# Two attention layers on one core: the third product of a split step in the second layer is issued one step later

## The chip, the cores and the metric

The kernel runs on one core of a Trainium2 chip. The metric is the device time of one execution in microseconds, the median of the runs shown.

## The reference, cut to what matters

Two self-attention layers run one after the other over x of shape (4, 64, 64, 256): 4 images of 4096 tokens with 256 channels. All is fp32, and each layer attends over all 4096 tokens of its image.

```python
# layer 0
q, k, v = x @ Wq + bq, x @ Wk + bk, x @ Wv + bv        # 32, 32 and 256 columns
x = gamma * (softmax(q @ k.T) @ v) + x
# layer 1
f, g, v = x @ Wf + bf, x @ Wg + bg, x @ Wh + bh        # 32, 32 and 128 columns
x = x + (softmax(g @ f.T) @ v) @ Wo + bo
```

## The kernel before, in words

`fast_path` (L239) does all the work; `general_path` (L76) is a fallback that these inputs don't take.

**Steps.** The attention is cut into steps `Step(b, l, j, i)` (L513): image, layer, query block, group of keys. In the second layer (l = 1) a query block has 512 queries, there are 8 such blocks an image (32 in all), and each has 16 steps of two key tiles of 128. A step has these parts:

- `scores` (L522): two TensorE matmuls (L529) write a 128 x 1024 tile `st` in PSUM, keys on the partitions. The pool `ps_st` (L261) has one buffer, so the next scores wait until ScalarE has read these. ScalarE then makes `p` = exp(st) (L541), and in a split step `high` = exp(st - a little), rounded to fp32r, ahead of it (L539).
- `cut_low` (L549): in a split step VectorE makes `low` = p - high (L552).
- `cut_both` (L554): in a split step VectorE makes `d` = high - 4096 low (L557). In the second layer `low` and `d` take turns in the same two buffers (tag "l"; L267, L551, L556).
- `add_up` (L561): VectorE adds p to the running sum for the softmax, except in steps 0, 3, 7, 10 and 13, for which POOL issues an adding DMA (L547).
- `products_second` (L585): the products of the exponentials with v, at L595. A step that isn't split has one product, "whole": two fp32 matmuls of p, into the accumulator `acc[1]`. A split step has three products of two fp32r matmuls each: "h" (high) and "l" (low), both into `acc[0]`, and "d" into `acc[1]`. At the end of the block the two accumulators are joined (`end_second`, L641), multiplied by Wo and divided by the sums.

In the second layer, steps 1, 4, 6, 9, 11 and 14 are split (`SPLIT1`, L68), the ten others are not. No two split steps are neighbours. In the first layer every step is split, with its own products at L577; it isn't touched.

**Order.** The main loop (L726 on) writes the steps out by hand, two ahead: at step n VectorE gets d(n), low(n+1) and the sum of n; then the scores of n+2, side work that `plan` (L693) puts at this step, and the products of n. The side work is the end of the block before (matmuls L658 and L659, in steps 1 to 4) and, in images 0 to 2, the projections of the next image (matmuls L421 and L463). `acc` is a fresh pair of PSUM banks for every block. The source gives the rank of the work; the framework sets each engine's order when the kernel is built, and the trace shows scores in the middle of the products of another step.

Of the kernel before, what the change touches and what calls it, by code (L numbers as in the profile page):

```python
# [238 lines left out]
def fast_path(ctx: ExitStack, tc: tile.TileContext, x, w0, w1, wo, bo, gamma, out, off):  # L239
# [26 lines left out]
    def wide(tag, name, dtype=F32):  # L266
        return work.tile([P, 2 * QB], dtype, tag=tag, bufs={"d": 1, "e": 1, "p": 3}.get(tag, 2), name=name)  # L267
# [226 lines left out]
    def load_q(b, l, j, cols=slice(0, QB), parts=None):  # L494
        if (b, l, j) not in q_t:
            q_t[b, l, j] = data.tile([P, QB], F32R, tag="q", bufs=2, name=f"q_{b}_{l}_{j}")
        parts = qk_dram[b, l, j].bitcast(F32R) if parts is None else parts
        load_rows(q_t[b, l, j][:, cols], parts, 0, (0, 0, 1, 1))

    def load_k(b, l, j, cols=slice(0, QB), parts=None):  # L500
        if (b, l, j) not in k_t:
            k_t[b, l, j] = data.tile([P, QB], F32R, tag="k", bufs=NB, name=f"k_{b}_{l}_{j}")
        parts = qk_dram[b, l, j].bitcast(F32R) if parts is None else parts
        load_rows(k_t[b, l, j][:, cols], parts, 1, (0, 1, 0, 1))
# [4 lines left out]
    def small(name):  # L509
        return work.tile([P, C], F32, tag="small", bufs=4, name=name)  # L510


    class Step:  # L513
# [71 lines left out]
        def products_second(self, acc, parts):  # L585
            v = v_t[self.b, self.i]
            for part in parts:
                p, v_part, which, first, last = {
                    "h": lambda: (self.high, v["h"], 0, self.i == SPLIT1[0], False),
                    "l": lambda: (self.low, v["l"], 0, False, self.i == SPLIT1[-1]),  # L590
                    "d": lambda: (self.d, v["d"], 1, self.first, self.last),
                    "whole": lambda: (self.p, v, 1, self.first, self.last),
                }[part]()
                for g in range(G[1]):
                    nc.tensor.matmul(  # L595
                        acc[which],
                        v_part[:, g, :],
                        p[:, g * QB : (g + 1) * QB],
                        start=first and g == 0,
                        stop=last and g == G[1] - 1,  # L600
                    )
# [39 lines left out]
    def end_second(b, j, acc, p_sum):  # L641
        key = f"{b}_{j}"
        o = []
        for h in range(QB // QB0):
            part = slice(h * QB0, (h + 1) * QB0)
            o.append(work.tile([P, W], F32, tag="o", name=f"o_{key}_{h}"))
            nc.scalar.activation(o[h][:, :QB0], acc[0][:, part], AF.Copy, scale=1.0 + EPS)
            nc.vector.tensor_add(o[h][:, :QB0], o[h][:, :QB0], acc[1][:, part])
        sums = work.tile([P, QB], F32, tag="sums", bufs=1, name=f"sums_{key}")
        nc.vector.tensor_add(p_sum, p_sum, moved_sums[b, j])  # L650
        nc.vector.tensor_add(sums, p_sum[:, :QB], p_sum[:, QB:])

        def output(t):
            def issue():
                tok = slice(t * P, (t + 1) * P)
                ps = side_psum(f"pso_{key}_{t}")
                part = o[t // NS][:, t % NS * P : (t % NS + 1) * P]
                nc.tensor.matmul(ps[:, :C], part, wo_sb, start=True, stop=True)  # L658
                nc.tensor.matmul(ps[:, C : C + 1], sums[:, tok], ones[:, :1], start=True, stop=True)  # L659
                n = (b * N + j * QB) // P + t  # L660
                nc.vector.reciprocal(inverse[:, 1, n : n + 1], ps[:, C : C + 1])

                y = small(f"y_{key}_{t}")
                nc.scalar.activation(y, ps[:, :C], AF.Copy, scale=inverse[:, 1, n : n + 1])  # L664
                row = j * QB + t * P
                nc.gpsimd.dma_start(out[b, row : row + P, :], y, accum_op=ALU.add)  # L666

            return issue

        return [output(t) for t in range(NT)]  # L670

    def run(units):
        for u in units:
            u()
# [9 lines left out]
    steps = [Step(b, l, j, i) for b in range(B) for l in range(2) for j in range(NQ[l]) for i in range(NI[l])]  # L684
# [6 lines left out]
    acc, p_sum, units = None, None, {}  # L691

    def plan(b, l, j, ends):  # L693

        units = {}

        def put(i, *some):
            units.setdefault(i, []).extend(some)

        if l == 0:  # L700

            if j >= 2:
                t, qk, v = project_units(b, 1, j - 2)
                put(0, t), put(4, qk), put(5, v)
            for n, u in enumerate(ends):
                put(1 + n, u)
            return units
        if j == 0:
            for n, u in enumerate(ends):
                put(1 + n, u)  # L710
            for n, h in enumerate((NH - 2, NH - 1)):
                t, qk, v = project_units(b, 1, h)
                put(6 * n, t), put(6 * n + 2, qk), put(6 * n + 3, v)
        else:
            for n, u in enumerate(ends):
                put(1 + n, u)
        if b + 1 < B:
            for h in range(NH):
                i = 12 + 7 * h - j * NI[1]
                for n, u in zip((0, 2, 3), project_units(b + 1, 0, h)):  # L720
                    if 0 <= i + n < NI[1]:
                        put(i + n, u)
        return units

    ends = bias_units()
    for n, s in enumerate(steps):  # L726
        b, l, j = s.b, s.l, s.j
        if s.first:
            units = plan(b, l, j, ends)
            acc = [  # L730
                ps_acc.tile([P, QB], F32, tag="acc", name=f"acc_{b}_{l}_{j}_{a}") for a in range(2 * NS if l == 0 else 2)
            ]
            if l == 1:
                p_sum = wide("d", f"p_sum_{b}_{j}")
        if l == 0 and s.last:
            x_res[b, j] = []
            for t in range(NS):
                x_res[b, j].append(small(f"x_res_{b}_{j}_{t}"))
                row = (j * NS + t) * P
                nc.sync.dma_start(x_res[b, j][t], x[b, row : row + P, :])  # L740
                nc.gpsimd.tensor_add(x_res[b, j][t], x_res[b, j][t], bv)  # L741

        ahead = steps[n + 3] if n + 3 < len(steps) else None
        if ahead is not None and ahead.first:
            k = (ahead.b, ahead.l, ahead.j * (QB0, QB)[ahead.l] // QB)
            if k not in q_t:
                load_q(*k)
        if b == l == j == 0 and s.i == 5:
            load_q(0, 0, 0, slice(QB0, QB), qk_dram[0, 0, 0].bitcast(F32R)[:, :, :, QB0:])
        after, later = (steps[n + k] if n + k < len(steps) else beyond for k in (1, 2))  # L750

        early = []
        if b == l == j == 0 and s.i + AHEAD < NB:
            early = [project_units(0, 0, 2 * (s.i + AHEAD) + k) for k in range(2)]
            run([u[0] for u in early])

        s.cut_both()
        after.cut_low()
        s.add_up(p_sum)
        todo = units.get(s.i, [])  # L760

        if l == 1:
            later.scores()
            run(todo)
            s.products_second(acc, ("h", "l", "d") if s.split else ("whole",))
        else:
            for half, what in ((0, "h"), (0, "l"), (1, "h")) if s.last else ((0, "h"), (1, "h")):
                s.products_first(acc, half, what)
            for half in () if s.last else (0, 1):
                s.products_first(acc, half, "l")  # L770
            if early:
                run(early[0][1:] + early[1][1:])
            later.scores()
            run(todo)
            for half, what in ((0, "d"), (1, "l"), (1, "d")) if s.last else ((0, "d"), (1, "d")):
                s.products_first(acc, half, what)

        over = (min(s.i + 2, NI[l] - 1) + 1) * G[l] // NT if j == NQ[l] - 1 else 0
        while keys and halves.get(keys[0]) == 2 and (keys[0][:2] == (b, l) or keys[0][2] < over):
            load_k(*keys.pop(0))  # L780
        if s.last:
            ends = end_first(b, j, acc) if l == 0 else end_second(b, j, acc, p_sum)
# [70 lines left out]
```

## Time and profile before

| what | value |
|---|---|
| median of 3 runs | 3232.82 us (3232.46 to 3236.61) |
| the profiled execution, its own time | 3232.26 us |
| its span in the trace | 3230.1 us, 2.2 us less |
| granted TensorE clock | 0.997 |
| busy: TensorE, VectorE, ScalarE, POOL | 98%, 83%, 66%, 28% |
| second layer: first whole product, image 0 and last d product, image 3 | 521.2 us and 3207.9 us after the start |
| one query block of the second layer, image 3 (3093.42 to 3132.65) | 39.2 us |

Times in the profile are microseconds from the start of the span unless marked ns. PE is the TensorE matmul, PEld its weight load, DVE VectorE, ACT ScalarE, SP the engine whose queue issues DMAs. A group's line gives the source line, engine, operation, output and inputs, shape and count, then busy time, mean ns of one, and the idle time of the engine just before, with what ended it. A matmul's record is longer than the distance to the next one, since matmuls are pipelined; a weight load carries the wait for its matmul's data, and the idle time before it is shown in brackets. Below, d(6) stands for the d product of step 6, whole(7) for the whole product of step 7, and so on; score 0 and score 1 at a block's end belong to the next block.

### The profile page before, as it was taken

The numbers are of one execution on the slowest core, as the hardware profiler recorded it, in microseconds if no ns is written. First come the engines' busy times: TensorE is split into PE (matmuls) and PEld (weight loads), VectorE is DVE, ScalarE is ACT, GpSimd is POOL, SyncE is SP. The second block draws the span as 40 slices with busy tenths as digits, with TensorE's granted clock in tenths as the row PEclk, the third lists the DMA queues.
The fourth block names the chain that finished last, engine by engine and source line by source line (L and its number), as shares of the span: only waits on it lengthen the run. The fifth ranks groups of instructions, "written<-read, shape, count | busy, mean of one in ns | idle before, by whom it ended". The sixth has DMA issues, their size and how long they took to land.

```text
span 3230.1 us, 54167 instructions
## 1 busy us (share of the span) xinstructions
PE 3159.7 (98%) x19908; PEld 2653.3 (82%) x19908; DVE 2679.5 (83%) x3237; ACT 2146.8 (66%) x2835; POOL 898.9 (28%) x1108
## 2 busy tenths in 40 slices
PE   8999999999999999999999999999999999999997
PEld 7999997666799999666689999966668999995554
DVE  7888888888788888888878888888888888887775
ACT  7666666767666666677766666667776666666664
POOL 5222223222422223322232222422233222232221
PEclk9999999999999999999999999999999999999999
DMA  4111214555421122555531111345562121134443
GB/s 120 45 45 48 52 46 105 105 102 105 93 50 46 46 52 54 107 107 103 110 76 47 45 47 47 73 101 108 103 117 61 42 52 48 45 87 89 85 87 66
DMA packets 391391, 239.49 MB, mean 74 GB/s; under 512 B 266672, under 2 KB 355248, under 8 KB 391120
## 3 DMA queue, kind: packets, MB, share of 16 engines
q0 software_dynamic: 68160, 134.86, 21.4%
q1 hardware_dynamic: 322048, 100.76, 13.0%
q8 instruction: 161, 2.64, 0.3%
q14 instruction: 110, 0.90, 0.1%
q10 hardware_dynamic: 912, 0.33, 0.0%
HBM read 82.58 MB, written 67.11 MB: 46 GB/s over the span
## 4 chain that ended last, share of the span: by engine, by line
PE 83%; DVE 6%; issue 4%; ACT 4%; DMA 2%; SPq 1%; POOL 0%; DVEq 0%; ACTq 0%; POOLq 0%
PE acc L577 44%; PE acc L595 18%; PE st L529 13%; PE psv L463 4%; DVE d L557 2%; DVE low L552 2%; ACT p L541 2%; PE psqk L421 2%; PE pso L658 1%; ACT high L539 1%; DMA squares<-x_dram 1%; SPq L279 1%; DMA squares<-in_x 1%; PE pso L659 0%; DMA p_sum_moved<-p 0%
## 5 line engine op out<-in xcount | busy, mean ns | idle before, releaser
L539 ACT ACTIVATE high<-st,down 128x1024 fp32r<-128x1024 f32 x704 | 786.2, 1117 | 734.5 <-PE st L529 532.8
L541 ACT ACTIVATE p<-st 128x1024 f32<-128x1024 f32 x1024 | 1045.8, 1021 | 230.8 <-PE st L529 225.3
L552 DVE TENSOR_TENSOR low<-p,high 128x1024 fp32r<-128x1024 f32 x704 | 937.5, 1332 | 192.4 <-ACT p L541 191.7
L557 DVE SCALAR_TENSOR_TENSOR d<-low,high 128x1024 fp32r<-128x1024 f32 x704 | 865.6, 1230 | 235.2 <-PE acc L577 232.3
L529 PE MATMUL st<-q,k 128*128 128x256 f32 (+1 forms) x3072 | 742.9, 349 | 10.0 <-ACT p L541 6.6
L595 PE MATMUL acc<-p,v 128*128 128x512 f32 x1280 | 614.7, 594 | 0.0
L529 PEld LDWEIGHTS st<-q,k 128*128 128x128 f32 x3072 | 454.4, 189 | 187.8 <-ACT p L541 122.7
L577 PE MATMUL acc<-v0d,d 128*128 128x258 f32 x4096 | 593.6, 284 | 3.1 <-DVE d L557 2.8
L577 PE MATMUL acc<-v0h,high 128*128 128x258 f32 x4096 | 590.8, 284 | 1.2 <-ACT high L539 1.2
L577 PE MATMUL acc<-v0l,low 128*128 128x258 f32 x4096 | 589.0, 283 | 0.1
L577 PEld LDWEIGHTS acc<-v0h,high 128*128 128x128 f32 x4096 | 535.3, 190 | 3.1 <-issue 1.4
L577 PEld LDWEIGHTS acc<-v0d,d 128*128 128x128 f32 x4096 | 530.4, 189 | 6.1 <-DVE d L557 5.3
L577 PEld LDWEIGHTS acc<-v0l,low 128*128 128x128 f32 x4096 | 532.9, 190 | 0.6 <-DVE low L552 0.3
L634 POOL TENSOR_TENSOR x_res<-x,bo 128x256 f32<-128x256 f32 x128 | 198.7, 1552 | 877.8 <-DVE x L623 877.7
L595 PEld LDWEIGHTS acc<-p,v 128*128 128x128 f32 x1280 | 236.3, 189 | 148.8 <-issue 123.2
L570 DVE TENSOR_TENSOR p_sum<-p_sum,p 128x1024 f32<-128x1024 f32 x288 | 350.3, 1216 | 8.2 <-ACT p L541 5.8
L547 POOL DMA_DIRECT2D p_sum_moved<-p x128 | 113.1, 884 | 527.0 <-ACT p L541 425.5
L492 POOL DMA_DIRECT2D q<-qk_dram x256 | 127.9, 510 | 323.7 <-PE st L529 318.5
L463 PE MATMUL psv<-wv,xT 128*128 128x128 f32 (+1 forms) x1024 | 202.2, 330 | 1.8 <-DVE v0d L481 1.4
L741 POOL TENSOR_TENSOR x_res<-x_res,bv 128x256 f32<-128x256 f32 x128 | 181.5, 1419 | 66.6 <-DMA x_res<-in_x 66.0
L463 PEld LDWEIGHTS psv<-wv,xT 128*128 128x128 f32 x1024 | 158.4, 191 | 32.6 <-issue 14.6
L666 POOL DMA_DIRECT2D out<-y x128 | 116.7, 930 | 243.0 <-ACT y L664 220.1
(100 smaller groups left out, 2411.7 us busy)
## 6 DMA issues: line engine op xcount, KB each, us to landing
p_sum_moved<-p POOLq DMA_DIRECT2D x160, 512.0 KB, 4.6
x_res<-in_x SPq DMA_DIRECT2D x128, 128.0 KB, 2.1
qk_dram<-qk_parts SPq DMA_DIRECT2D x128, 128.0 KB, 1.9
x_dram<-x SPq DMA_DIRECT2D x128, 128.0 KB, 1.7
out<-x_res SPq DMA_DIRECT2D x128, 128.0 KB, 1.7
squares<-x_dram SPq DMA_DIRECT2D x512, 32.0 KB, 1.9
out<-y POOLq DMA_DIRECT2D x128, 128.0 KB, 3.4
q<-qk_dram POOLq DMA_DIRECT2D x252, 64.0 KB, 2.3
```

What stands on the lines that cost most here:

```text
L463: nc.tensor.matmul(ps[:, t, :], xT[key][:, c, t * P : (t + 1) * P], wv[l][:, c, :], start=(c == 0), stop=(c == NCC - 1),)
L492: nc.gpsimd.dma_start(dst[n * D : (n + 1) * D, :], parts[h, which])
L529: nc.tensor.matmul(st[:, g, :], k_t[b, l, kt // NT][:, kt % NT * P : (kt % NT + 1) * P], q_t[b, l, j * n // QB][:, q0 : q0 + n], start=Tru ...
L539: nc.scalar.activation(self.high, s_flat, AF.Exp, bias=down)
L541: nc.scalar.activation(self.p, s_flat, AF.Exp)
L552: nc.vector.tensor_sub(self.low, self.p, self.high.bitcast(F32))
L557: nc.vector.scalar_tensor_tensor(self.d, self.low.bitcast(F32), -UP, self.high.bitcast(F32), ALU.mult, ALU.add)
L570: nc.vector.tensor_add(p_sum, p_sum, self.p)
L577: nc.tensor.matmul(acc[2 * s + which][:, :W], p[:, g * QB0 + s * P : g * QB0 + (s + 1) * P], v0[self.i][v][:, g, :], start=self.first and ...
L595: nc.tensor.matmul(acc[which], v_part[:, g, :], p[:, g * QB : (g + 1) * QB], start=first and g == 0, stop=last and g == G[1] - 1,)
L634: nc.gpsimd.tensor_add(x_old[s], x_new[s], bo_sb)
L741: nc.gpsimd.tensor_add(x_res[b, j][t], x_res[b, j][t], bv)
```

## The change

In a split step of the second layer, "d" is taken out of the call that issues the products. It is issued in the next step instead, which is never split: behind that step's whole product, or ahead of it where that step is the last of the block (step 15, for the d of step 14). The whole product of step 0 still opens acc[1] and that of step 15 still closes it; the flags of d, which depended on being the first or last step, become constants.

```diff
-                    "d": lambda: (self.d, v["d"], 1, self.first, self.last),
+                    "d": lambda: (self.d, v["d"], 1, False, False),
...
         if l == 1:
             later.scores()
             run(todo)
-            s.products_second(acc, ("h", "l", "d") if s.split else ("whole",))
+
+            behind = steps[n - 1] if not s.first and steps[n - 1].split else None
+            if s.last and behind:
+                behind.products_second(acc, ("d",))
+            s.products_second(acc, ("h", "l") if s.split else ("whole",))
+            if not s.last and behind:
+                behind.products_second(acc, ("d",))
```

## The prediction

> **What bounds the kernel now.** I read the page first (busy shares, then the chain that ended last), then the groups by form, then who waited for whom on TensorE, then one stretch of the second layer in order of time.
>
> ```profile
> PE 3159.7 (98%) x19908; PEld 2653.3 (82%) x19908; DVE 2679.5 (83%) x3237; ACT 2146.8 (66%) x2835; POOL 898.9 (28%) x1108
> PE 83%; DVE 6%; issue 4%; ACT 4%; DMA 2%; SPq 1%; POOL 0%; DVEq 0%; ACTq 0%; POOLq 0%
> ```
>
> TensorE is busy nearly all the time and is 83% of the chain, so only its idle time can be won. The next lines are three groups of second-layer products (columns: count, then busy us and mean ns of one, then idle time before), and one line of the waits on TensorE.
>
> ```profile
> L595 PE MATMUL acc<-p,v 128*128 128x512 f32 x1280 | 614.7, 594 | 0.0
> L595 PE MATMUL acc<-high,v 128*128 128x512 f32 x384 | 146.3, 461 | 2.0 <-ACT high L539 2.0
> L595 PE MATMUL acc<-d,v 128*128 128x512 f32 x384 | 130.3, 420 | 25.7 <-DVE d L557 23.6
> ...
> PE acc L595 <- DVE d L557: 23.6, 40, 1.5
> ```
>
> The moved product is the only one on L595 with a wait worth naming. Its 23.6 us is too low, because matmul records overlap. In the trace the end of one 512-column fp32r matmul follows the end of the one before by 0.231 us, and each of the four passes that a whole fp32 product (two matmuls) leaves by 0.428 us. What the ends lie further apart is idle. Summed by that rule over the trace, counting gaps over 40 ns, TensorE idles ahead of the d products by split step (32 query blocks): step 1 2.8 us, 4 none, 6 7.9, 9 7.2, 11 10.2, 14 15.4. The first five make 28.1 us: 15.7 in images 0 to 2 together, 12.4 in image 3, which has no projection work for a next image beside it.
>
> One block of image 3 in order of time (start, duration, what; idle before):
>
> ```profile
> 3115.17 1.22 DVE L557 SCALAR_TENSOR_TENSOR d<-low,high 128x1024 fp32r<-128x1024 f32 x1
> 3115.45 0.63 PE L595 MATMUL acc<-low,v 128*128 128x512 f32 x2
> ...
> 3116.44 0.30 PEld L595 LDWEIGHTS acc<-d,v 128*128 128x128 f32 x2 [0.80 <-DVE d L557]
> 3116.44 0.73 PE L595 MATMUL acc<-d,v 128*128 128x512 f32 x2 [0.36 <-DVE d L557]
> 3116.71 1.02 ACT L541 ACTIVATE p<-st 128x1024 f32<-128x1024 f32 x1
> ...
> 3117.01 1.88 PE L595 MATMUL acc<-p,v 128*128 128x512 f32 x4
> ...
> 3118.33 1.03 PE L529 MATMUL st<-q,k 128*128 128x512 f32 x2
> ...
> 3120.47 0.30 PEld L529 LDWEIGHTS st<-q,k 128*128 128x128 f32 x2 [0.63 <-ACT p L541]
> 3121.24 1.03 ACT L541 ACTIVATE p<-st 128x1024 f32<-128x1024 f32 x1 [0.82 <-PE st L529]
> 3121.31 0.30 PEld L595 LDWEIGHTS acc<-d,v 128*128 128x128 f32 x2 [0.54 <-DVE d L557]
> ```
>
> See that d(9) is made by VectorE from 3115.17 on, that TensorE has done low(9) and stands, and that the whole product of step 10, whose p has been ready for some time, follows only after it. See also the second limit: a score waits for ScalarE's p, because st has one buffer (L261, L526), so scores and exponentials alternate. In this block (3093.42 to 3132.65, 39.2 us) seven of the 16 scores start 0.16 us after the p before them ended; there ScalarE, not TensorE, sets the pace.
>
> **What the Trainium skill says.** "TensorE: Matmul & The Clock Gate", Architectural detail: TensorE pulls weight loads ahead of matmuls, but matmuls stay in order, and VectorE and ScalarE are strict FIFO. The trace agrees: at 3116.44 the load for d waits, and the ready whole product behind does not pass it. So only the order of the instructions can fill that hole. "Perfetto Trace Analysis", Tensor Engine Instruction: the end of a matmul record is estimated, which is why I use spacing; the trace agrees, records of 395 ns (median for low) lie 231 ns apart. "PSUM — Partial Sum Buffer", The four PSUM rules: the first matmul of a group clears, the others add. Step 0 opens and step 15 closes acc[1], both whole products and neither split, so the changed flags on d do nothing.
>
> **The change part by part.**
>
> Work removed or added: none. 384 d matmuls stay, 6 x 32 pairs at 0.462 us. No DMA is issued by the moved call, so the POOL and SP queues keep their order; POOL's copies of p (L547) hang on ScalarE. On TensorE it is moved past the scores and side units of step n+1 and its whole product.
>
> Steps 1, 4, 6, 9, 11: d(n) goes behind the whole product of n+1. What stood behind the wait was the scores of n+3 and that whole product, 1.71 us. That is longer than the longest wait seen (1.2 us in these steps), so where p is ready the hole is filled. What is late next is the score. I walk the block above with the durations of the trace: p's end to score 0.155, score's end to ScalarE 0.22, VectorE's end to d 0.16.
> - Step 6: low(6) stops at 3109.17 and d(6) waits 0.39. But score 9 can't start before 3110.11, since p(8) ends at 3109.95. Half of whole(7), 0.857, fits in between. Score 9 gains nothing; score 10 gains 0.13, its slack (start 3113.15, p(9) ended 3112.86).
> - Step 9: scores and low(9) are 0.13 earlier, low(9) ends 3115.78. Whole(10) runs to 3117.50. p(11), also 0.13 earlier, ends 3117.60, so score 12 starts 3117.75 instead of 3118.72: 0.97 gained. d(9) follows it.
> - Step 11: score 13 hangs on p(12), so 3119.60 instead of 3120.57. Whole(12) goes before d(11) and ends 3121.78; score 14 starts then instead of 3122.73: 0.95 kept, nothing more.
> - Step 14: d(14) stays ahead of whole(15) and only changes places with the score and side units of step 15. Its 15.4 us hangs on VectorE's low(14), sum, d(14), which start when p(14) ends. I count zero of it, with bounds 0 and 15.4.
> So the block gains 0.96 of the 1.40 us that its d products idle in the five steps: 69%. Step 4 has no wait; step 1 has 0.9 us or less an image.
>
> Image 3: 8 blocks x 0.96 = 7.7 us. Images 0 to 2: the idle times sit in fewer blocks beside projection matmuls; 0.69 x 15.7 = 10.8. Sum 18.5 us.
>
> Buffers: d and low share tag "l" with two buffers (L267), so d(6) is written where d(4) was, and d(11) where d(9) was. In the block d(4)'s product ended at 3105.56 and VectorE began d(6) at 3108.19, 2.6 us later. With whole(5) in between (1.71), and the 0.46 of d(4) itself behind it, it ends about 3107.8 plus 0.16: margin 0.2. Where side units stand in step 5 or 10 (a query/key projection, 0.47 us by four matmuls 0.117 apart, or a value projection, 8 x 0.215 = 1.72 us), VectorE waits, and low(n) and the sums queue behind that. By plan (L717 to L722) such units fall there in four of the eight blocks of images 0 to 2, 12 cases. Nothing in before shows this wait. From below 0; a gain is excluded, since a later release helps nobody. From above about 1.7 us each, 20 us. Much of it is cover, since d itself now has 1.71 us more time. I take 2 us.
>
> Order: the engines don't run in source order. Scores stand in the middle of whole products in the trace, so the build ranks what is ready and the source gives only the rank. In none of the 192 split steps does a whole product pass an earlier d, so d blocks whole as read above, and after the change d(n) stays behind whole(n+1). Where exactly the scores fall is unknown; I price it at zero, 0.2 us a block either way (6 us).
>
> Sum: 3232.26 (profiled execution: span 3230.1 and 2.2 around it) - 18.5 + 2.0 = 3215.8; the median shown is 0.56 above that execution: 3216.3.
>
> **The rivals.**
> 1. Part of the wait is won (above): 3216. For: the filler is ready and long enough. Chance 0.44.
> 2. All of it: the chain from the scores has more slack in the blocks with projections than in the one I walked. 3232.8 - 28.1 = 3204.7. Against: the scores that start right behind p. Chance 0.11.
> 3. The wait moves: at each d the score waits for ScalarE instead, as in step 6, or the build leaves d where it was because it counts it as ready. Then 3232, within 0.2%. For: ScalarE is the releaser of seven scores of 16. Chance 0.19.
> 4. Slower: VectorE's d(6) and d(11) wait for the released buffer of d(4) and d(9), and low(9), low(14) and the sums queue behind. There are 64 such pairs; from 18.5 / 64 = 0.29 us on average they eat the gain. At 0.4 us, 25.6 - 18.5 = 7 us slower: 3240. For: margin 2.6 to 0.2 us, VectorE busy 83%. Against: in the block VectorE stands idle 8.4 us for ScalarE. Chance 0.26.
>
> **Numbers.** Faster 0.55 (1 and 2), same 0.19, slower 0.26; the bound of 0.2% (6.5 us) is about what a measurement of this kernel can tell from no change. The range reaches from most of case 2 (3206) to case 4 at its price (3240); some 0.05 lies below, 0.13 above. The likeliest case alone has 3209 to 3223, by the 6 us of order and the buffer wait.
>
> **What would show it.** Right: idle time ahead of d in steps 1, 6, 9 and 11 falls below 5 us in sum, the image-3 block shrinks from 39.2 to about 38.3 us, score 12 starts within 0.3 us of the end of p(11), and step 14 keeps its wait. Wrong: the wait of scores for p (6.6 us in the view of who waited for whom) grows by as much as d's falls (case 3), or d L557 shows a wait for acc L595, which it never does now (case 4).

## The result, and the profile after

| | before | after |
|---|---|---|
| median of 8 runs each | 3232.64 us (3230.55 to 3236.61) | 3225.61 us (3222.68 to 3227.84) |
| ratio after / before | | 0.9976, 95% interval 0.9965 to 0.9986 |
| the profiled execution, its own time | 3232.26 us | 3224.69 us |
| its span, granted TensorE clock | 3230.1 us, 0.997 | 3222.8 us, 0.997 |
| second layer, first whole(0) to last whole(15), images 0, 1, 2, 3 | 337.4, 337.0, 337.7, 317.4 us | 336.1, 336.5, 337.7, 313.9 us |
| one query block of image 3, whole(0) to the next whole(0) | 39.2 us | 38.54 us |

The change wins 7.0 us, 0.2%; 16.5 us had been forecast. The second layer gives 5.3 us in the profiled executions, 1.8 us in images 0 to 2 and 3.5 us in image 3. The four stretches ahead of the images' second layers, start and first layer, were 1.1, 1.3 and 0.4 us shorter and 0.9 us longer; the change does not touch them.

First the same lines of the page of after (busy shares, then the chain):

```profile
PE 3162.2 (98%) x19908; PEld 2651.3 (82%) x19908; DVE 2675.7 (83%) x3237; ACT 2147.8 (67%) x2835; POOL 897.1 (28%) x1108
PE 91%; DVE 3%; ACT 2%; issue 2%; DMA 1%; POOL 0%; SPq 0%; ACTq 0%; DVEq 0%; POOLq 0%
```

The number of TensorE instructions is unchanged. VectorE's share of the chain fell from 6% to 3%, TensorE's rose from 83% to 91%. Next the second-layer products of after by form (count, busy us and mean ns, idle before):

```profile
L595 PE MATMUL acc<-p,v 128*128 128x512 f32 x1280 | 623.1, 597 | 0.0
...
L595 PE MATMUL acc<-d,v 128*128 128x512 f32 x384 | 168.7, 511 | 4.4 <-DVE d L557 4.4
L595 PE MATMUL acc<-high,v 128*128 128x512 f32 x384 | 138.3, 436 | 0.4 <-ACT high L539 0.4
```

The idle time of the d group fell from 25.7 to 4.4 us. Its busy time rose from 130.3 to 168.7 us for the same 384 matmuls: a d now starts right behind a fp32 pass and its record overlaps that one. By the spacing rule of the prediction (gaps over 40 ns), the idle time ahead of d fell from 43.5 to 5.5 us, all of it in step 14; in steps 1, 4, 6, 9 and 11 no such gap is left. So the change does what it says. What it does not do is turn 38 us of filled holes into 38 us. The view of who waited for whom tells why. These are the weight loads of before (us, times, longest):

```profile
PEld st L529 <- ACT p L541: 122.7, 345, 1.6
PEld acc L595 <- DVE d L557: 52.5, 70, 2.0
```

and these the weight loads of after:

```profile
PEld st L529 <- ACT p L541: 162.8, 385, 1.5
PEld acc L595 <- DVE d L557: 7.1, 8, 2.0
```

The wait for d lost 45.4 us and the wait of the scores for p gained 40.1 us. On the matmuls themselves d went from 23.6 to 4.4 us and the score from 6.6 to 13.4 us. By the spacing rule TensorE's idle time ahead of the second layer's scores grew from about 35 to about 60 us.

Where the change works as it was walked can be seen in one block of image 3, steps 9 to 12 of after (start, duration, what):

```profile
3070.02 1.22 DVE L557 SCALAR_TENSOR_TENSOR d<-low,high 128x1024 fp32r<-128x1024 f32 x1
3070.18 0.63 PE L595 MATMUL acc<-low,v 128*128 128x512 f32 x2
...
3070.64 1.88 PE L595 MATMUL acc<-p,v 128*128 128x512 f32 x4
...
3071.44 1.02 ACT L541 ACTIVATE p<-st 128x1024 f32<-128x1024 f32 x1
...
3071.96 0.79 PE L595 MATMUL acc<-d,v 128*128 128x512 f32 x1
...
3072.59 0.42 PE L529 MATMUL st<-q,k 128*128 128x512 f32 x1
```

VectorE makes d(9) from 3070.02 on, and TensorE goes from low(9) straight into whole(10), then d(9). p(11) ends at 3072.46 and score 12 starts 0.13 us behind it.

### The profile page after: what moved, and what is told of

The parts are those of the page before. It is cut to its first block, busy times and chain, and to the rows that moved or that the text cites. A ratio compares the mean times of both kernels' runs of the same rounds, so it can differ in the third digit from the quotient of the medians.

```text
span 3222.8 us, 54179 instructions
## 1 busy us (share of the span) xinstructions
PE 3162.2 (98%) x19908; PEld 2651.3 (82%) x19908; DVE 2675.7 (83%) x3237; ACT 2147.8 (67%) x2835; POOL 897.1 (28%) x1108
## 3 DMA queue, kind: packets, MB, share of 16 engines
q1 hardware_dynamic: 322048, 100.76, 13.1%
## 4 chain that ended last, share of the span: by engine, by line
PE 91%; DVE 3%; ACT 2%; issue 2%; DMA 1%; POOL 0%; SPq 0%; ACTq 0%; DVEq 0%; POOLq 0%
PE acc L577 45%; PE acc L595 23%; PE st L529 15%; PE psv L463 4%; PE pso L658 2%; PE psqk L421 2%; ACT p L541 1%; DVE low L552 1%; DVE d L557 1%; ACT high L539 1%; PE pso L659 0%; DMA squares<-x_dram 0%; DMA k<-qk_parts 0%; DMA gamma<-in_L_conv_gamma 0%; POOL k L492 0%
## 5 line engine op out<-in xcount | busy, mean ns | idle before, releaser
L557 DVE SCALAR_TENSOR_TENSOR d<-low,high 128x1024 fp32r<-128x1024 f32 x704 | 865.4, 1229 | 235.5 <-PE acc L577 231.8
L529 PE MATMUL st<-q,k 128*128 128x256 f32 (+1 forms) x3072 | 737.1, 348 | 17.4 <-ACT p L541 13.4
L595 PE MATMUL acc<-p,v 128*128 128x512 f32 x1280 | 623.1, 597 | 0.0
```

Of the source, the lines that this page charges most:

```text
L529: nc.tensor.matmul(st[:, g, :], k_t[b, l, kt // NT][:, kt % NT * P : (kt % NT + 1) * P], q_t[b, l, j * n // QB][:, q0 : q0 + n], start=Tru ...
L557: nc.vector.scalar_tensor_tensor(self.d, self.low.bitcast(F32), -UP, self.high.bitcast(F32), ALU.mult, ALU.add)
L595: nc.tensor.matmul(acc[which], v_part[:, g, :], p[:, g * QB : (g + 1) * QB], start=first and g == 0, stop=last and g == G[1] - 1,)
```

## The experiments

**How the blocks were read.** A block's time is the distance from its first whole(0) to the next block's. All `st` tiles share one buffer, so the block can be written as 16 round trips, from the start of a score over its exponentials to the end of its p, plus 0.155 us, plus what the next score starts later than that. A score that waits gets its record early, so its start is taken as the end of its first matmul less 0.395 us, the length of a record that didn't wait. A round trip is 1.84 us in a plain step and 2.90 in a split one; ten and six of them make 35.8 us, and no block of image 3 came under that. What is above it is mostly **lateness** of scores; the rest is round trips that take longer. For the block of before (39.23 us), by score: 4: 0.22, 6: 0.99, 7: 0.39, 10: 0.14, 12: 0.84, 14: 0.30, 15: 0.14, 1: 0.17, 2: 0.14, in all 3.3 us.

**The theories.** A, with which the first group went in: idle time ahead of d is what a move wins, and what is missing of it is lost at the block's end, where the build now puts score 1 ahead of d(14). The rival, which became theory C: filled holes count only where they make a score less late, and the build's new order makes other scores late, so each block should come out as its round trips and its lateness. Images are timed in one profiled execution of each kernel. Images 0 to 2 of the two kernels at the end of group 3, where nothing in them differs from before, came out 0.6 us shorter and 1.2 us longer than before in sum, so differences near 1 us say little there. Line numbers in some of these kernels are one higher than in before, for an added line.

### Group 1: one step at a time, and the block's end

`e1_only14` moves d(14) alone, `e3_only9` d(9) alone:

```diff
+MOVED_D = (14,)        # e3_only9: (9,)
-            behind = steps[n - 1] if not s.first and steps[n - 1].split else None
+            behind = steps[n - 1] if not s.first and steps[n - 1].split and steps[n - 1].i in MOVED_D else None
...
-            s.products_second(acc, ("h", "l") if s.split else ("whole",))
+            s.products_second(acc, (("h", "l") if s.i in MOVED_D else ("h", "l", "d")) if s.split else ("whole",))
```

> Only d(14) is moved (into step 15, ahead of its whole product), the other five stay in their own steps. Theory A (the moves of 6, 9 and 11 win, and the move of 14 loses because the planner now lets score 1 of the next block, which must wait for p(0), go ahead of d(14)): the image-3 block is 39.2 to 39.5 us, that is not shorter than before, and the time is 3232 to 3241. Theory B (the score-exponential alternation alone sets the time; where d stands is of no account): 39.2 us and 3232 as before.

Measured: 3233.80 us beside 3231.76 of before, ratio 1.0006 (0.9998 to 1.0015); image-3 block 39.31 us. No gain, as expected.

> Only d(9) is moved. Theory A (my step-by-step walk): nearly all of an image-3 block's gain comes from step 9, where the score of step 12 was 0.84 us late behind d(9): block 38.3 to 38.7 us against 39.2 before, and 3226 to 3231 in all. Theory B or an even spread over the five moved steps: 0.1 to 0.2 us a block, 39.0 to 39.1, time as before.

Measured: 3224.26 us, ratio 0.998 (0.9971 to 0.9988); image-3 block 38.18 us, both a little below theory A's ranges; image 3 309.9 us. Scores 12, 14 and 15 are not late at all; score 0 is, by 0.34. One move wins more in image 3 (7.5 us) than all six (3.5 us, or 5.2 us without a stretch at half speed, see the last section), and 1.05 us a block, close to the 0.97 walked for step 9. So the gain of step 9 is there, and the other five moves take a part of it back.

`e2_d14_first` is after, with score 1 bound behind d(14):

```diff
-            later.scores()
-            run(todo)
...
-                behind.products_second(acc, ("d",))
+                with tc.issue_after(behind.products_second(acc, ("d",)).ins):
+                    later.scores()
+            else:
+                later.scores()
+            run(todo)
```

> The changed kernel, with one order fixed: in step 15 the scores of the next block's step 1 may not be issued on TensorE ahead of d(14). Theory A: score 1's wait of 1.38 us an image-3 block shrinks to below 1.1, the block from 38.55 to about 38.3 us, the time from 3225.6 to about 3217. Theory B: the wait only changes its name, block 38.5 us and 3225.

Measured: 3228.61 us, ratio 0.9987 (0.9981 to 0.9994); image-3 block 39.37 us, a miss. With score 1 held back, the build put the first half of the next block's whole(0) ahead of d(14); it waits for the same p(0), and score 1 starts 1.32 us late. This is the end of the block in after itself, without that edit:

```profile
3081.46 0.66 ACT L647 ACTIVATE o<-acc 128x256 f32<-128x256 f32 x2 [0.25 <-PE acc L595]
3081.68 1.22 DVE L557 SCALAR_TENSOR_TENSOR d<-low,high 128x1024 fp32r<-128x1024 f32 x1
3082.03 1.02 ACT L541 ACTIVATE p<-st 128x1024 f32<-128x1024 f32 x1
...
3083.11 0.73 PE L529 MATMUL st<-q,k 128*128 128x512 f32 x2 [1.11 <-ACT p L541]
3083.68 0.62 PE L595 MATMUL acc<-d,v 128*128 128x512 f32 x2
```

d(14) is ready at 3082.90 and score 1, ahead of it in the queue, holds it until p(0) is done at 3083.05. By the spacing rule TensorE stands 1.38 us there (before: 1.09, at d(14)). Yet score 1 is on time: it could not start sooner. ScalarE's two copies at 3081.46 look like the cause of p(0)'s late start, so `e4_o_vector` gives them to VectorE:

```diff
-            nc.scalar.activation(o[h][:, :QB0], acc[0][:, part], AF.Copy, scale=1.0 + EPS)
+            nc.vector.tensor_scalar(o[h][:, :QB0], acc[0][:, part], 1.0 + EPS, None, ALU.mult)
```

> The changed kernel, with the two copies of acc[0] at a block's end (0.77 us, between p(15) and p(0) on ScalarE) made on VectorE instead. If score 1's wait of 1.38 us hangs on ScalarE's queue (p(0) behind the two copies), it falls to about 0.6, the image-3 block to about 37.8 us and the time to about 3205 to 3215. If it hangs on something else (VectorE, or the order alone), block 38.5 us and 3225, or longer where VectorE is full in images 0 to 2.

Measured: 3227.95 us, ratio 0.9989 (0.9982 to 0.9995); image-3 block 38.56 us, the second case. The wait stayed at 1.38 us: the copies lie in the time in which score 0 runs, and p(0) waits for that. So the largest idle time of TensorE left in the block costs nothing, and theory A fell.

### Group 2: which moves make which scores late

The same edit with other lists, `(6,)`, `(9, 11)` and `(1, 4)`; `e8_9_spread` moves d(9) alone and puts the four output units of the block before (L658, L659, and y at L664) at steps 1, 6, 11 and 14 in place of 1 to 4:

```diff
-                put(1 + n, u)
+                put((1, 6, 11, 14)[n], u)
```

> Only d(6) is moved. Theory C (new: a block takes the time of its 16 round trips score - exponential - next score, which the single st buffer lines up, plus what each score starts late; idle time of TensorE ahead of a d counts only where it makes a score late): d(6)'s own wait of 0.39 us made no score late, so it wins nothing by itself; but in this kernel's order on TensorE the score of step 12 stands in the middle of whole(10), 0.86 us earlier than before, so the 0.84 us by which it was late go: image-3 block 38.3 to 38.5 us, d(9) still waiting, longer than before. Theory A (the block falls by the idle time ahead of the moved d): 38.8 to 38.9 us.

> d(9) and d(11) are moved. Theory A (idle time ahead of d adds up): better than d(9) alone by the 0.37 us an image-3 block that d(11) idled, 37.8 to 37.9 us against 38.2. Theory C: in its order the score of step 14 comes behind whole(12) again, some 0.3 us late, and score 1 is split around d(14): 38.4 to 38.6 us, that is slower than d(9) alone, and 3224 to 3227 in all.

> Only d(1) and d(4) are moved; no d ahead of which TensorE idles in image 3. Theory A: nothing in image 3 (39.2 us), up to 2.3 us in images 0 to 2 together. Theory C: the 0.39 us that score 7 is late go over to score 9, so 39.0 to 39.3 us; in images 0 to 2 scores 4 and 6 come later behind side work as in the changed kernel, 0 to 4 us slower; in all 3230 to 3236.

> Only d(9) is moved, and the four output units of the block before are put in steps 1, 6, 11 and 14 instead of 1 to 4 (second to eighth block of an image). Theory C: the score of step 6, late by 0.99 us in every image-3 block behind these units, comes on time: block 37.3 to 37.6 us against 38.2, and 3207 to 3216 in all. Theory A (TensorE's own work and its waits for d set the time): the work is the same and no d waits less, so 38.2 us and 3224.

| kernel | us (before 3232.88) | ratio (95%) | image-3 block, us | images 0, 1, 2; 3, us | scores that are late, image 3 |
|---|---|---|---|---|---|
| after | 3225.61 (3232.64) | 0.9976 (0.9965 to 0.9986) | 38.54 | 336.1, 336.5, 337.7; 313.9 | 3: .33, 4: .20, 5: .09, 6: .99, 9: .39, 14: .33 |
| e5_only6 | 3222.34 | 0.9965 (0.9952 to 0.9978) | 38.27 | 335.7, 335.7, 336.7; 311.9 | 4: .22, 6: 1.00, 7: .39, 12: .12, 14: .18, 15: .14, 1: .17, 2: .14 |
| e6_9_11 | 3234.21 | 1.0004 (0.9996 to 1.0013) | 38.78 | 338.5, 337.6, 338.7; 318.3 | 4: .19, 5: .39, 6: .56, 7: .41, 10: .14, 14: .57, 2: .14 |
| e7_1_4 | 3230.20 | 0.999 (0.9981 to 0.9998) | 39.32 | 334.4, 335.7, 335.2; 320.4 | as before, without 7 |
| e8_9_spread | 3221.24 | 0.9964 (0.995 to 0.9977) | 37.47 | 337.4, 337.0, 338.0; 304.3 | 4: .22, 5: .13, 8: .17, 10: .13, 0: .34, 2: .14 |

The image-3 times of three of these executions hold time in which TensorE's clock was at half (last section): 3.4 us in the image's first block in `e5_only6`, 6.8 us there in `e6_9_11` and `e7_1_4`, and 3.4 us at the end of the image in `e6_9_11`. Their first blocks took 44.61, 45.72 and 45.37 us, against 43.19 in before. The blocks of the table come after the first and are free of it.

For image 3, the block of `e5_only6` came just below theory C's range and far from A's: d(6) alone removes 0.72 of the 0.84 at score 12, and not by filling the hole of step 9, as this stretch of it shows:

```profile
3074.38 0.73 PE L596 MATMUL acc<-d,v 128*128 128x512 f32 x2 [0.49 <-DVE d L558]
...
3074.95 1.02 PE L596 MATMUL acc<-p,v 128*128 128x512 f32 x2
...
3075.59 0.84 PE L530 MATMUL st<-q,k 128*128 128x512 f32 x2
```

TensorE still stands 0.49 us for d(9), but the build now puts score 12 behind two of the four passes of whole(10); in before (the block shown with the prediction) it comes behind all four. The block of `e6_9_11` came above both: with d(11) moved too, score 14 is 0.57 late and score 5 0.39, and d(14) stands between the two matmuls of score 1, which makes round trip 1 3.36 in place of 2.90 us. Its total missed by more (3224 to 3227 expected): images 0 to 2 lost 2.7 us, and 10.2 us of its profiled execution ran at half clock in image 3. The granted clock is 0.996 in eight of its twelve runs, against one in 26 of before beside it, so more time at half clock comes back from run to run. `e7_1_4` takes away the lateness of score 7 and gets nothing in the block: d(6) now stands between the two matmuls of score 9, and ScalarE starts high(9) only after the second:

```profile
2990.50 0.50 PE L530 MATMUL st<-q,k 128*128 128x512 f32 x1 [0.18 <-ACT p L542]
2990.84 0.63 PE L596 MATMUL acc<-d,v 128*128 128x512 f32 x2
2991.31 0.39 PE L530 MATMUL st<-q,k 128*128 128x512 f32 x1
```

Round trip 9 takes 3.36 in place of 2.90 us. So a score can be held up in two ways: it starts late, or it is cut in two. Images 0 to 2 of `e7_1_4`, expected up to 4 us slower, came 6.8 us faster. `e8_9_spread` hit for the block (37.3 to 37.6 expected) by taking the output units from the steps ahead of score 6. In after, score 6 stands behind a whole product:

```profile
3055.75 1.02 ACT L541 ACTIVATE p<-st 128x1024 f32<-128x1024 f32 x1 [0.54 <-PE st L529]
...
3056.12 1.96 PE L595 MATMUL acc<-p,v 128*128 128x512 f32 x4
...
3057.52 1.02 PE L529 MATMUL st<-q,k 128*128 128x512 f32 x2
```

p(5) ends at 3056.77, but the four passes of a whole product, queued behind output matmuls (L658, L659), run until about 3057.9: 0.99 us late. In `e8_9_spread` score 6 has its data last:

```profile
3056.94 1.02 ACT L542 ACTIVATE p<-st 128x1024 f32<-128x1024 f32 x1 [0.94 <-PE st L530]
...
3058.06 0.69 PE L530 MATMUL st<-q,k 128*128 128x512 f32 x2
```

p ends at 3057.96 and the score follows at once. Its score 9 is cut in two as in `e7_1_4`. Its total missed (3207 to 3216 expected): image 3 won 13.1 us, images 0 to 2 nothing.

### Group 3: the two best put together, and idle time that is free

Images 0 to 2 gained most with d(1) and d(4) moved (6.8 us in `e7_1_4`), image 3 with `e8_9_spread` (13.1 us). `e9_by_image` gives each its own:

```diff
-                put(1 + n, u)
+                put((1, 6, 11, 14)[n] if b == B - 1 else 1 + n, u)
...
+            moved = (9,) if b == B - 1 else (1, 4)
```

> A version put together from the runs so far by the block times of their traces: d(1) and d(4) moved in images 0 to 2, d(9) alone moved in image 3 and the output units there spread over steps 1, 6, 11 and 14. If the sections add up as theory C has it (image 3 wins about 13 us as in the run with spread units, images 0 to 2 about 6 as in the run with d(1) and d(4)): 3232 - 19 = 3213, within 3210 to 3217. If a section's time depends on what comes ahead of it, less: 3217 to 3226.

Measured: 3214.02 us beside 3231.81, ratio 0.9947 (0.9933 to 0.996); images 334.4, 335.4, 335.3 and 305.3 us. It is 17.8 us faster than before and the fastest of all kernels here.

Two kernels then put unused work into before, in the blocks of image 3: four fp32r matmuls of low and v into a side bank that nobody reads, 4 x 0.231 = 0.92 us a block. In `e10_extra14` they stand in step 14 between low and d, where TensorE idles; in `e11_extra2` in step 2, where it does not.

```diff
+            for g in (0, 1, 0, 1):
+                nc.tensor.matmul(ps, v_t[self.b, self.i]["l"][:, g, :],
+                                 self.low[:, g * QB : (g + 1) * QB], start=True, stop=True)
```

> The kernel before, with work added in image 3: four more 512-column fp32r matmuls (0.92 us) a block into a PSUM tile that nobody reads, in step 14 between low(14) and d(14), where TensorE idles 1.1 to 1.3 us. Theory A (TensorE at 98% sets the time): block 39.2 to 40.1 us, 7 us in all. Theory C (only late scores count, and none gets later here): block 39.2 to 39.4 us, at most 1 us in all, though TensorE works 7.4 us more.

> The same four matmuls a block in image 3 of the kernel before, but in step 2 behind its whole product, where the next score (step 5) starts as soon as p(4) is there. Theory C: score 5 and all behind it become late by what the 0.07 us of wait doesn't cover, about 0.85 us a block that is not won back by the idle times at d(6), d(9) or d(14): block 40.0 to 40.1 us, 3238 to 3240 in all. If idle times further on can take it up (1.4 us at d(6), d(9), d(11) alone): 39.2 to 39.4 us.

Measured: `e10_extra14` 3231.13 us, ratio 0.9998 (0.999 to 1.0007); `e11_extra2` 3234.86 us, ratio 1.001 (1.0001 to 1.0018), less than the 3238 to 3240 expected. Its profiled execution (span 3237.9 us) is the second slowest of the twelve; what the others have that it lacks is not shown. The same block in before, then `e10_extra14`, then `e11_extra2` (window; its length in us; busy us of PE, PEld, DVE, ACT and POOL with instructions; clock, DMA share, GB/s):

```profile
3053.31:3092.57 39.26, 37.66 (x126) 21.82 (x124) 28.82 (x31) 24.64 (x29) 9.55 (x13) 1.00 0.46 87
```

```profile
3053.72:3092.98 39.26, 38.41 (x130) 22.55 (x129) 28.76 (x31) 24.61 (x29) 9.54 (x13) 1.00 0.46 87
```

```profile
3057.69:3097.80 40.11, 38.51 (x129) 22.65 (x128) 28.79 (x31) 24.59 (x29) 9.52 (x13) 1.00 0.45 86
```

TensorE went from 37.66 to 38.41 us of 39.26 and the block did not grow: the wait ahead of d(14) shrank from about 1.1 to about 0.4 us and no score came later. The same work in step 2 made score 5 late by 0.86 us and the block 0.85 us longer. This is theory C from the other side: what can be taken from an idle time, or put into it, is worth what it does to the next late score.

### Group 4: do the moves add up in images 0 to 2?

Beside before (1012.1 us for the three images), d(1) and d(4) gave -6.8, d(6) -4.0, d(9) -1.2, d(14) +1.2, and d(9) with d(11) +2.7. Without 11 and 14, d(1), d(4), d(6) and d(9) together should give about -12. `e12_without_11_14` is `e9_by_image` with `(1, 4, 6, 9)` in place of `(1, 4)`.

> As the version put together by image, with d(6) and d(9) moved in images 0 to 2 as well, so that there the five moves stand without those of 11 and 14. In the traces, images 0 to 2 together came out against before at -6.8 us with d(1) and d(4) moved, -4.0 with d(6), -1.2 with d(9), +3.9 where d(11) was added to d(9), +1.2 with d(14). If the moves of 11 and 14 are what ate the gain in images 0 to 2 and the rest adds up: images 0 to 2 at -8 to -12 us, 3207 to 3212 in all. If the moves don't add up because each one lets the order be planned anew: -2 to -7 us, 3213 to 3219.

Measured: 3214.61 us beside 3232.29, ratio 0.9944 (0.9931 to 0.9958), not told apart from `e9_by_image`; images 0 to 2 -6.7 us. The moves of 6 and 9 add nothing to those of 1 and 4. A part of the -12 had been counted more than once: from the end of p(15) to the end of whole(15) at the end of an image it is 4.56 us in before and 4.05 in the kernels with d(1) and d(4), d(6), or d(9), and in this one. These 1.5 us over three images stand in each of the three differences and can be had once only, so about -9 was to be expected. The shortfall is 2.3 us.

## Why the prediction was right in sign and wrong in size, point by point

**What held.** The idle time in steps 1, 6, 9 and 11 fell below 5 us in sum (no gap over 40 ns is left). Score 12 starts within 0.3 us of p(11)'s end (0.13). The buffer wait, rival 4, is there and negligible. This is the view of VectorE's d (L557) in after, under the heading that its engine sat idle until:

```profile
  PE acc L577: 231.8, 275
  PE acc L595: 1.3, 3
```

Three waits for a second-layer product, 1.3 us in all, against the 2 us taken and the 20 us of its upper bound. In after no score or product of the second layer waits for POOL.

**The step that failed: "Images 0 to 2: the idle times sit in fewer blocks beside projection matmuls; 0.69 x 15.7 = 10.8."** Measured: 1.8 us, so 9.0 us of what is missing is here. The factor 0.69 came from one block in which two late scores stood behind the two idle d products. It was then multiplied with idle time, which is not the quantity that counts. Summed over each of images 0 to 2, the lateness of the scores went from 40.7, 40.7 and 41.4 us to 39.3, 39.0 and 40.0, and the round trips from 295.8, 295.0 and 295.1 to 295.4, 295.6 and 295.9. Holes were filled; the scores hardly came earlier: 4.5 us less lateness, 1.0 us more in round trips. Another 1.6 us went at the ends of the three images, where d(14) and with it whole(15) end 0.5 us later behind p(15). Within rounding that leaves the 1.8 us. By score, over these three images, lateness fell at 5 (16.5 to 14.2), 7 (10.5 to 6.4), 8 (5.9 to 2.5), 10 (6.9 to 4.2) and 12 (4.8 to 1.3), and rose at 4 (10.0 to 14.5), 6 (17.8 to 21.9) and 11 (4.7 to 8.2). This is rival 3, in which the wait moves to the scores: it was given 0.19 and took most of the gain.

**"Order: ... I price it at zero, 0.2 us a block either way."** This term failed too. In image 3 the block lost 0.69 us in place of 0.96. Scores 7, 10, 12, 15, 1 and 2 came on time, 1.8 us in all. Against that, score 3 is now 0.33 late and score 9 0.39, which they never were, and a copy y stands in front of p(4):

```profile
3052.45 1.11 ACT L539 ACTIVATE high<-st,down 128x1024 fp32r<-128x1024 f32 x1 [1.01 <-PE st L529]
3053.47 0.47 ACT L664 ACTIVATE y<-pso,inverse 128x256 f32<-128x256 f32 x1
3053.82 1.02 ACT L541 ACTIVATE p<-st 128x1024 f32<-128x1024 f32 x1
```

In before, p(4) follows high(4) with nothing between, and y comes after it:

```profile
3058.82 1.11 ACT L539 ACTIVATE high<-st,down 128x1024 fp32r<-128x1024 f32 x1 [0.73 <-PE st L529]
3059.83 1.02 ACT L541 ACTIVATE p<-st 128x1024 f32<-128x1024 f32 x1
3060.73 0.48 ACT L664 ACTIVATE y<-pso,inverse 128x256 f32<-128x256 f32 x1
```

In after round trip 4 is 3.21 in place of 2.90 us. These three make 1.03 us a block, five times the bound given. `e3_only9` has the same gain of step 9 without these, and a block of 38.18; it is no exact control, since its own order leaves scores 7 and 10 late as in before and makes score 0 late by 0.34.

**"Image 3: 8 blocks x 0.96 = 7.7."** Measured: 3.5 us. Six blocks gave 0.62 to 0.73 each, 4.1 us in sum. The first of the image took 0.45 longer (43.19 to 43.64). The last is 0.13 longer (38.79 to 38.91) in this profiled execution: at its end the whole product runs at half speed, see below, for 1.7 us; `e4_o_vector`, with the same walk and without that stretch, has 37.22 there. With it taken out, image 3 would stand near 5.2 us.

**Step 14: "I count zero of it."** The number was right and the reason incomplete, and the sign given for it, that step 14 keeps its wait, did not come. Its idle time fell from 15.4 to 5.5 us, but only because score 1 took the place of d(14) in the queue and waits there: TensorE's idle time ahead of score 1 rose from 5.6 to 18.4 us over the run. The walk took d(14) and score 15 to change places, not a score of the next block. `e10_extra14` shows why it costs nothing.

**What stays open.** In images 0 to 2 the build re-plans the order for every set of moves, in the presence of the next image's projections, and no run held the rest of that order fixed. That the moves of 6 and 9 give nothing beside those of 1 and 4 is shown (`e12_without_11_14`), though the shortfall of 2.3 us is not far above what unchanged images differ by; which displaced score eats which gain there is not shown. Nor is it shown why the block of `e2_d14_first` has score 6 on time and scores 5, 7 and 9 late. A second buffer for `st`, which might lift the bound itself, was not tried: the page "PSUM — Partial Sum Buffer" of the Trainium skill, section Specifications (TRN2), has eight banks of 512 fp32 values in a partition, which no run here tests, and the pools of this kernel hold all of them by their shapes (`st` two, four accumulators, two side tiles).

## What to carry to other kernels

Where a loop turns around one buffer, as the scores of this kernel do, price idle time on the busiest engine at the next member of that loop: count what the next score starts late or is held up between its matmuls, not what TensorE idles. 0.92 us of extra work a block was free in one hole and cost 0.85 us in a place without one, on an engine that was busy 96% of that block. In a framework that ranks and reorders, moving one call re-plans everything around it: measure each move alone, expect that the sum of the moves is not the move of the sum, and keep only those that pay (here 17.8 us for a choice by image together with the spread output units, against 7.0 for all six).

## What the runs showed of the hardware that was not expected

At the end of after's last block TensorE stood for d(14), and the whole product behind it took twice its time:

```profile
3198.64 0.30 PEld L595 LDWEIGHTS acc<-d,v 128*128 128x128 f32 x2 [1.97 <-DVE d L557]
...
3199.21 3.57 PE L595 MATMUL acc<-p,v 128*128 128x512 f32 x4
```

Four passes take 1.88 us elsewhere and 3.57 here, and the granted clock of these 3.4 us is 0.50 (columns as in group 3, the clock third from the end):

```profile
3199.20:3202.60 3.40, 3.40 (x5) 0.98 (x3) 1.75 (x2) 0.00 (x0) 0.00 (x0) 0.50 0.00 0
```

The Trainium skill, "TensorE: Matmul & The Clock Gate", Part 1: The HAM clock gate, has two states of the clock, full and half, switched by how busy TensorE was in windows of about 3.4 us. The half speed and the length agree. The wait ahead was shorter than such a window, 1.97 us. Of the eight profiled executions with this wait there, two have the slow product (after, and `e6_9_11` with 3.53 us); in the six others (before, `e1_only14`, `e2_d14_first`, `e4_o_vector`, `e7_1_4`, `e11_extra2`) it takes 1.88 us. What decides is not shown.

Such stretches lie elsewhere too: in before at 92.5 us, and in the first block of image 3 in `e2_d14_first` and `e5_only6` (3.4 us each) and in `e6_9_11` and `e7_1_4` (6.8 us each). This is the one of `e7_1_4`:

```profile
2926.30:2933.10 6.80, 5.16 (x11) 3.33 (x11) 5.80 (x6) 3.62 (x5) 2.55 (x5) 0.50 0.16 39
```

The first block took 1.4 to 2.5 us more there than in before (`e1_only14`, without one, 0.7 us more). One stretch of 3.4 us moves an execution by up to 1.7 us, a quarter of the gain measured here. That the order of the work brings it on is likely for `e6_9_11`, by its granted clock in most runs, and not shown. Read the granted clock of a stretch before a difference in it is put down to waits.
